# Expert tiles with two images' rows moved ahead in the last series, and their results turned beside the last tile

## The chip, the cores and the metric

The kernel runs on one core of a Trainium2 chip. The core has five engines that run side by side, each with its own queue of instructions: TensorE (PE, matmuls; PEld is its loading of weights), VectorE (DVE), ScalarE (ACT), GpSimd (POOL) and SyncE (SP). Transfers are issued from queues: SP's and ACT's go through the hardware queues, POOL's indirect ones through a software queue. The metric is the time of one execution on the device in microseconds, as a median over runs; less is better. The trace of one profiled execution shows where that time goes.

## What is computed

Four images of 256 channels and 32 x 32 positions pass through one layer: a mixer (selective scans, convolutions, attention) and then a mixture of experts over all 4096 positions (tokens). Only the second matters here:

```python
t = t + ffn(layernorm(t))              # t: 4096 rows of 256
# ffn, with 8 experts, two for each row:
gate_logits = xf @ Wg + bg
top_w, top_i = jax.lax.top_k(gate_logits, 2)
top_w = jax.nn.softmax(top_w, axis=-1)
for e in range(8):
    h = gelu(xf @ W1[e] + b1[e])       # 256 -> 1024
    out = out + w_dense[:, e:e+1] * (h @ W2[e] + b2[e])   # 1024 -> 256
```

All values are float32. The result goes back to the layout with the channels first.

## The kernel before

The images' mixers run one after the other. As each image is done, `dispatch` normalises its rows, picks the two experts of each and writes each row twice into a DRAM buffer XS, which has a region for every expert; a row of XS also carries its token's number and its weights. The rows before the experts are written to a second DRAM buffer, Y. XS grows by image, so the first rows of an expert's region are those of the earlier images.

The experts work by tiles of 256 rows of one expert. A plain tile loads its rows from XS and its expert's W1 and W2 (2 MB), turns the rows with four transposes on PE, and does 32 h matmuls (L2259) with a Gelu on ACT for each of eight blocks, then 32 y matmuls (L2272) in two row blocks of 128. DVE adds the bias (`ys`, L2286) and multiplies by the row's weight (L2291), and POOL adds each row block to its tokens' rows of Y with an indirect transfer that accumulates (L2299). The adds of a tile wait for those of the tile before it. A wide tile has 320 rows, in three blocks.

Tiles come in four series, `SERIES = (8, 8, 21, 8)`. Series 0 starts when two images' rows are counted, series 1 with three; both take whole tiles alone. Series 3 (`WIDE`) and series 2 (`rest`) come when all four images are counted: wide tiles take an expert's last rows, series 2 the plain tiles that are left. Which expert and which row each tile begins with is worked out on the chip by DVE in a table (`series` L2078, `wide_series` L2040, `table` L1991), and SP reads it into registers (`values_load`) ahead of each tile's loads. Of series 2 the last 9 tiles, of series 3 the last 4, are kept for rare splits of the rows: they stand in a conditional in `run` (L2141) and are skipped here. So 32 tiles run: 8, 8, and then a wide one followed by three plain ones, four times.

`tiles` (L1378) writes the order out by hand. The program is emitted step by step by generators (each `yield` lets the others emit), and each engine executes its instructions strictly in the order in which they were emitted. While tile n is emitted, `ahead(n + 1, at)` (L1438) is called at each of its steps: at step 0 it emits the table if it is wanted, the next tile's rows (L2160) and weights (L2194, L2196); from step 5 on, within the y matmuls, the next tile's transposes (`front`, L2218). Both tables of the last series are emitted in the first such call after image 3's places are known (L1440). Weights are held for two tiles.

After the last tile, `judge` (L1597) tests sums that the scans left, to decide on a second pass of the whole network (the conditional at L71, skipped here). Then `run` (L2113) opens a new pool, reads `any_late` into registers on all engines, skips the late tiles, and calls `bring_back` (L2310) for each of the four images: two loads of half an image from Y (L2315, 512 KB each), 16 transposes (L2324), eight copies out of PSUM shared by DVE (L2330) and ACT (L2328), and two stores to the output issued by ACT (L2331). Two `o` buffers are used in turn.

Of the kernel before, what the change touches and what calls it, by code (L numbers as in the profile page):

```python
# [14 lines left out]
P = 128  # L15
C = 256
# [32 lines left out]
LATE, LATE_WIDE = 9, 4  # L49

# [25 lines left out]
def network(  # L76
# [71 lines left out]
    with tc.tile_pool(name="w_conv", bufs=1) as wp, tc.tile_pool(  # L148
# [239 lines left out]
        def a8(name):  # L388
            return act8.tile([P, NC2, N], F32, tag="a8", name=name)
# [7 lines left out]
        def a4(name):  # L397
            return act4.tile([P, N], F32, tag="a4", name=name)
# [978 lines left out]

        def tiles():  # L1378
# [5 lines left out]
            between = (experts.SERIES[rest] - LATE) // some  # L1384
            for i in range(some):
                order.append((wide, i))
                order += [(rest, i * between + k) for k in range(between)]
# [50 lines left out]
            def ahead(n, at):  # L1438

                if experts.placed and wide not in tables:  # L1440
                    tables[wide] = experts.series(wide, temp)
                    tables[rest] = experts.series(rest, temp)
                if n == len(order):
                    return
                if n in got and len(got[n]) > 4:
                    return
                if n in xs and n in got and at >= 5:
                    front(n)
                    return

                if known(n) and n not in tables_of:
                    table(n)
                if n not in xs and sent(n):
                    rows(n)
                if n not in got and known(n):
                    load(n)

            for n in range(len(order)):
# [19 lines left out]
                for at, _ in enumerate(experts.tile(  # L1478
                    n, s, got[n], hs,
                    act4.tile([P, len(experts.blocks(s)), C], F32, tag="a4", name=f"ys_{n}"),  # L1480
                )):
                    if at < 4:
                        loaded[0] = None
                    ahead(n + 1, at)
                    yield T.get(("pace",), 1)
# [54 lines left out]
        with tc.manual_schedule(engines=ALL):  # L1540
# [53 lines left out]
            start(one_by_one(joined(B - 1), around(B - 1), sent_off(B - 1)))  # L1594
            drain()

    if not shifted:  # L1597
        with tc.tile_pool(name="judge", bufs=1) as jp:
            most = jp.tile([P, 1], F32, name="most")
            for i, span in enumerate((SPAN, INVERSE)):  # L1600
                nc.vector.tensor_scalar(sums[:, i, :], sums[:, i, :], span, None, ALU.is_lt)
            nc.vector.tensor_reduce(most, sums.rearrange("p a b -> p (a b)"), AX.X, ALU.min)

            nc.vector.tensor_scalar(most, most, 1.0, None, ALU.is_lt)
            any_ = ps_tile("any")
            nc.tensor.matmul(any_[0:1, 0:1], ones_mean[:, 0:1], most, start=True, stop=True)
            nc.vector.tensor_scalar(bad, any_[0:1, 0:1], 0.0, None, ALU.is_gt)

    experts.run(experts.tables)
# [11 lines left out]
class Experts:  # L1621
# [19 lines left out]
    def __init__(self, ctx, tc, psum, B, b1, ident, eps5, ones_mean, Wg, bg, W1, W2, b2, out):  # L1641
# [74 lines left out]
        self.read = []  # L1716
        self.apart = m0.tile([P, 1], F32, name="apart")
# [249 lines left out]
    def count_up(self, s, temp):  # L1967

        nc, K, n = self.nc, self.NTOK // self.T, self.SERIES[s]
        steps = temp(f"steps_{s}", [P, NE, K])  # L1970
        base = {self.WIDE: 0, self.WIDE - 1: REST}.get(s, self.T - 1)
        nc.gpsimd.iota(
            steps, [[0, NE], [self.T, K]], base=base,
            channel_multiplier=0, allow_small_or_imprecise_dtypes=True,
        )
        which = temp(f"which_{s}", [P, n, NE])
        nc.gpsimd.iota(
            which, [[1, n], [0, NE]], base=0, channel_multiplier=0,
            allow_small_or_imprecise_dtypes=True,
        )  # L1980
        self.numbers[s] = steps, which

# [8 lines left out]
    def table(self, temp, keep, name, n, ntile, which, done=None):  # L1991
# [3 lines left out]
        ends = keep(f"ends_{name}", [P, 1, NE])  # L1995
        nc.vector.tensor_tensor_scan(
            ends[:, 0, :], self.every[:, 0:NE], ntile[:, 0, :], 0.0, ALU.mult, ALU.add
        )
        starts = temp(f"starts_{name}", [P, 1, NE])
        nc.vector.tensor_tensor(starts, ends, ntile, ALU.subtract)  # L2000
        S = [P, n, NE]
# [7 lines left out]
        nc.vector.tensor_scalar(expert, expert, float(NE - 1), None, ALU.min)  # L2009
# [7 lines left out]
        nc.vector.tensor_tensor(which, which, self.region[:, 0:1, :].to_broadcast(S), ALU.add)  # L2017
# [13 lines left out]
    def use(self, s, ends):  # L2031

        late = LATE_WIDE if s == self.WIDE else LATE
        over = self.used[s] = self.m0.tile([P, 1], mybir.dt.int32, name=f"over_{s}")
        self.nc.vector.tensor_scalar(
            over, ends[:, :, NE - 1 : NE].rearrange("p a e -> p (a e)"),
            float(late - self.SERIES[s]), 0.0, ALU.add, ALU.max,
        )

    def wide_series(self, temp):  # L2040
# [34 lines left out]
        self.use(s, ends)  # L2075
        return table

    def series(self, s, temp):  # L2078
# [7 lines left out]
        if s == self.WIDE - 1:  # L2086
            assert before + n == self.NTILE
            table, _, ends = self.table(temp, self.kept, s, n, self.left, which, self.done)
            self.use(s, ends)
            self.any_late = self.m0.tile([P, 1], mybir.dt.int32, name="any_late")  # L2090
            nc.vector.tensor_tensor(
                self.any_late, self.used[s], self.used[self.WIDE], ALU.add
            )
            return table
# [18 lines left out]
    def run(self, tables):  # L2113

        tc, nc = self.tc, self.nc
        with tc.tile_pool(name="moe2", bufs=2) as m2:
            def load(v):
                return nc.values_load(
                    v[0:1, 0:1], min_val=0, max_val=sum(self.SERIES),
                    skip_runtime_bounds_check_because="made from counts of at most NTOK rows",  # L2120
                )

            def late_tile(s, i):
                j, W = f"{s}_{i}", self.width(s)
                w1 = m2.tile([P, NC2, DFF], F32, tag="w1", name=f"w1_{j}")
                w2 = m2.tile([P, NHC, C], F32, tag="w2", name=f"w2_{j}")
                got = self.load(
                    s, i, tables[s], [w1], [w2], m2.tile([P, C], F32, tag="b2", name=f"b2_{j}")
                )
                xs = m2.tile([P, len(self.blocks(s)), self.ROW], F32, tag="xs", name=f"xs_{j}")  # L2130
                self.rows(s, i, tables[s], xs)
                got += self.front(
                    j, s, i, tables[s], xs, m2.tile([P, NC2, W], F32, tag="xT", name=f"xT_{j}")
                )
                for _ in self.tile(
                    j, s, got, [m2.tile([P, NHC, W], F32, tag="hs", name=f"hs_{j}")],
                    m2.tile([P, len(self.blocks(s)), C], F32, tag="ys", name=f"ys_{j}"),
                ):
                    pass

            with tc.If(load(self.any_late) > 0):  # L2141
                for s, late in ((self.WIDE - 1, LATE), (self.WIDE, LATE_WIDE)):
                    n = self.SERIES[s]
                    with tc.If(load(self.used[s]) > 0):
                        for i in range(n - late, n):
                            late_tile(s, i)
            for b in range(self.B):
                self.bring_back(b, m2)
# [96 lines left out]
    def tile(self, j, s, got, hs, ys):  # L2245
# [9 lines left out]
        for k0 in range(0, NHC, each):  # L2255
# [9 lines left out]
            if k0 % 2 == 0:  # L2265
                yield
        for t, n in blocks:
            if t % 2 == 0:
# [9 lines left out]
            if parts > 1:  # L2278
# [3 lines left out]
                nc.vector.tensor_tensor(ys[0:n, t], yp[0:n, 0:C], other, ALU.add)  # L2282
            elif t % 2 or t == len(blocks) - 1:
# [6 lines left out]
        for t, n in blocks:  # L2290
            nc.vector.tensor_scalar(  # L2291
                ys[0:n, t, :], ys[0:n, t, :], wgt[0:n, t, :], None, ALU.mult
            )

        added = []
        for t, n in blocks:
            if t:
                nc.gpsimd.memset(self.apart, 0.0)
            ins = nc.gpsimd.indirect_dma_start(  # L2299
                out=self.Y[:, :],  # L2300
                out_offset=bass.IndirectOffsetOnAxis(ap=dest[0:n, t, :], axis=0),
                in_=ys[0:n, t, :], in_offset=None, compute_op=ALU.add,
            )
            for other in added:
                self.tc.declare_no_dep(ins.ins, other.ins, reason="no two share a row")
            self.follow(ins, self.added, "a row may be added to by both")
            added.append(ins)
        self.added = added

    def bring_back(self, b, m2):  # L2310

        nc, NT = self.nc, self.NT
        y = m2.tile([P, NT, C], F32, tag="yy", name=f"yy_{b}", bufs=self.B)
        for h in range(2):
            nc.sync.dma_start(  # L2315
# [3 lines left out]
        o = m2.tile([P, NC2, N], F32, tag="o", name=f"o_{b}")  # L2319
# [112 lines left out]
```

## Time and profile before

| what | us |
|---|---|
| median of three runs | 2202.95 |
| lowest, highest | 2195.85, 2204.05 |
| the profiled execution | 2182.24 |
| its span, first to last instruction | 2180.3 |
| PE busy | 1937.3 (89%) |
| DVE busy | 1533.4 (70%) |
| ACT busy | 1212.4 (56%) |
| POOL busy | 1048.1 (48%) |

The span is what the trace covers; the execution is 1.9 us longer. PE's busy time contains pipelined matmuls. A time such as 2151.22 is counted from the span's start. In a timeline a line has the start, the length, the engine, the line of the code, the operation and its tiles, how many in a row, and in brackets how long the engine had been idle and what released it. "SPq" and the like are the instructions of an engine's queue (issues of transfers, semaphores, branches), which are not counted as busy.

### The profile page before, as it was taken

How to read it: one execution, taken by the hardware profiler on the slowest of the kernel's cores; microseconds unless marked ns; L12 is line 12 of the kernel's file. 1: busy time of each engine (PE TensorE's matmuls, PEld its weight loads, DVE VectorE, ACT ScalarE, POOL GpSimd, SP SyncE). 2: the span in 40 equal slices, each digit the busy share in tenths (PEclk: the TensorE clock that was granted, in tenths of full speed). 3: DMA queues.
4: the chain of work that ended last, by engine and by line, in shares of the span. 5: the costliest groups of instructions: out<-in, count | busy, mean ns of one | idle time of the engine just before them, and what ended most of it. 6: DMA issues, size and time to landing. Idle time of an engine off the chain costs nothing. (4 is left out here: it accounts for less than half of the span.)

```text
span 2180.3 us, 28168 instructions
## 1 busy us (share of the span) xinstructions
PE 1937.3 (89%) x8690; PEld 874.4 (40%) x8690; DVE 1533.4 (70%) x2231; ACT 1212.4 (56%) x2272; POOL 1048.1 (48%) x930
## 2 busy tenths in 40 slices
PE   6778778999978999987789999768999999999995
PEld 2113112322212332222123223225642668888884
DVE  4989998857999988799898888985365356121211
ACT  4665657668668577776566776625168423222221
POOL 0887887712888740476977025752040013422221
PEclk8988999999999999998999999889999999999997
DMA  3565553401444421153634024454230166967665
GB/s 107 146 162 123 127 125 91 106 22 59 116 115 107 111 60 39 34 132 100 177 79 113 1 78 101 104 177 123 78 115 1 46 196 198 261 186 191 175 162 167
DMA packets 157087, 251.40 MB, mean 115 GB/s; under 512 B 34740, under 2 KB 101332, under 8 KB 156664
## 3 DMA queue, kind: packets, MB, share of 16 engines
q1 hardware_dynamic: 136560, 223.47, 37.8%
q0 software_dynamic: 12720, 17.32, 4.0%
q10 hardware_dynamic: 7640, 8.65, 1.2%
q8 instruction: 72, 1.18, 0.2%
q14 instruction: 95, 0.78, 0.1%
HBM read 137.22 MB, written 36.62 MB: 80 GB/s over the span
## 5 line engine op out<-in xcount | busy, mean ns | idle before, releaser
L744 POOL TENSOR_TENSOR dA<-hs,cs 128x512 f32<-128x512 f32 x512 | 683.2, 1342 | 374.8 <-DVE hs L736 315.8
L715 ACT ACTIVATE dA<-dts,A 128x512 f32<-128x512 f32 x512 | 358.7, 718 | 159.2 <-DMA dts<-dt 71.8
L754 PE MATMUL yp<-dA,quads 128*32 128x512 f32 x1024 | 290.0, 640 | 85.3 <-POOL dA L744 74.0
L2299 POOL DMA_INDIRECT Y<-ys,dest x68 | 108.8, 1601 | 507.6 <-DVE ys L2291 500.2
L1133 ACT ACTIVATE e<-st 128x512 f32<-128x512 f32 x512 | 263.8, 605 | 93.2 <-PE st L1123 85.8
L2264 ACT ACTIVATE hs<-h,b 128x256 f32<-128x256 f32 (+1 forms) x256 | 110.5, 478 | 334.7 <-PE h L2259 231.7
L725 DVE TENSOR_TENSOR dBu<-dts,bs 128x512 f32<-128x512 f32 x384 | 260.0, 678 | 49.8 <-PE bs L707 14.8
L736 DVE TENSOR_TENSOR_SCAN hs<-dA,last,dBu 128x512 f32<-128x512 f32 x192 | 243.7, 1269 | 3.3 <-PE yp L754 1.1
L2272 PE MATMUL y<-w,hs 128*128 128x256 f32 (+1 forms) x1088 | 244.6, 384 | 0.0
L2259 PE MATMUL h<-xT,w 128*128 128x256 f32 (+1 forms) x1024 | 237.4, 388 | 0.1
L736 DVE TENSOR_TENSOR_SCAN hs<-dA,dBu 128x512 f32<-128x512 f32 x192 | 232.0, 1208 | 3.7 <-PE av L1143 2.7
L1179 DVE TENSOR_TENSOR e<-e,e 128x512 f32<-128x512 f32 x256 | 170.0, 726 | 76.0 <-ACT e L1133 40.2
L2272 PEld LDWEIGHTS y<-w,hs 128*128 128x128 f32 (+1 forms) x1088 | 199.1, 190 | 36.3 <-issue 8.7
L2259 PEld LDWEIGHTS h<-xT,w 128*128 128x128 f32 x1024 | 194.5, 191 | 43.6 <-issue 11.0
L2222 DVE COPY xT<-xp 128x512 f32<-128x512 f32 (+1 forms) x36 | 23.3, 646 | 245.5 <-PE xp L2218 245.2
L707 PE MATMUL bs<-u,xpwT_s 128*32 128x512 f32 x1024 | 162.8, 652 | 34.9 <-DVE hs L736 15.1
L1123 PE MATMUL st<-qk 32*128 32x512 f32 x1024 | 174.8, 638 | 1.9 <-DVE hs L736 1.9
L754 PEld LDWEIGHTS yp<-dA,quads 128*32 128x32 f32 x1024 | 51.1, 114 | 298.1 <-POOL dA L744 194.1
L1169 PE MATMUL av<-e,v 128*32 128x512 f32 x1024 | 138.6, 604 | 0.0
L1123 PEld LDWEIGHTS st<-qk 32*128 32x128 f32 x1024 | 59.9, 183 | 116.7 <-issue 86.2
L1143 PE MATMUL av<-e,every 128*32 128x512 f32 x512 | 86.8, 594 | 4.1 <-DVE e L1179 4.1
L725 DVE TENSOR_TENSOR bs<-dts,bs 128x512 f32<-128x512 f32 x128 | 86.2, 674 | 0.7 <-DMA dts<-dt 0.7
(335 smaller groups left out, 2625.0 us busy)
## 6 DMA issues: line engine op xcount, KB each, us to landing
dts<-dt SPq DMA_DIRECT2D x512, 128.0 KB, 2.4
w<-in_W_dram SPq DMA_DIRECT2D x124, 512.0 KB, 3.9
cs<-cd SPq DMA_DIRECT2D x512, 64.0 KB, 2.1
xs<-XS SPq DMA_DIRECT2D x32, 260.0 KB, 4.2
xd<-xn SPq DMA_DIRECT2D x64, 128.0 KB, 3.0
xn<-in_x_dram SPq DMA_DIRECT2D x8, 512.0 KB
XL<-xl SPq DMA_DIRECT2D x8, 512.0 KB
xl<-XL SPq DMA_DIRECT2D x4, 1024.0 KB
```

Source lines behind the costliest of these rows:

```text
L707: nc.tensor.matmul(bs[r], xpwT_s[:, n, s : s + 1].to_broadcast([P, 32]), T[b, n, "u"][:, half(h)], start=True, stop=True,)
L715: nc.scalar.activation(dA, T[b, n, h, "dts", g][:, 0, :], AF.Exp, scale=A[:, g, n, q : q + 1])
L725: nc.vector.tensor_tensor(dBu, T[b, n, h, "dts", g][:, 1, :], T[b, n, h, "bs", q], ALU.mult)
L736: nc.vector.tensor_tensor_scan(hs, T[b, n, h, "dA", i], dBu, 0.0 if h == 0 else last, ALU.mult, ALU.add)
L744: nc.gpsimd.tensor_tensor(dA, hs, T[b, n, h, "cs", q], ALU.mult)
L754: nc.tensor.matmul(T[b, n, h, "yp"][ts(g, 32)], quads, T[b, n, h, "dA", q * GD + g], start=False, stop=(q == GS - 1),)
L1123: nc.tensor.matmul(sts[i], k[r, ts(kt, P)], q[r, half(h)], start=True, stop=not shifted)
L1133: nc.scalar.activation(es[i], sts[i], AF.Exp, scale=1.0 / HD**0.5)
L1169: nc.tensor.matmul(accs[0][ts(i, HD)], v8[:, kt, ts(4 * g + i, HD)], es[i], start=(kt == 0), stop=(kt == NK - 1),)
L1179: nc.vector.tensor_tensor(first[i], first[i], es[i], ALU.add)
L2259: nc.tensor.matmul(hp[:, i, :], w1(c, k0 + i), xT[:, c, :], start=(c == 0), stop=(c == NC2 - 1))
L2272: nc.tensor.matmul(yp[ts(k % parts, n), ts(t % 2, C)], hidden(k)[:, ds(t * P, n)], w2(k), start=(k < parts), stop=(k >= NHC - parts),)
```

## The change

The order of the last series is another: the first wide tile, then eight plain ones in a row (`EARLY = 8`), then four times a plain one after which, but for the last, a wide one comes. The eight are meant to hold all rows of images 0 and 1 (`SOON = 2`) that are left by then, so series 2 now ranks its tiles by two kinds for each expert: those with rows of the first two images, then the others. The table works with 16 kinds in place of 8. It is emitted in the call that follows the first wide tile's rows, and no longer beside the wide table. At the fifth step of the second tile after the eight (tile 26 of 0 to 31), images 0 and 1 are loaded from Y. They are turned and stored after the last tile and ahead of the conditional. If more than eight tiles turn out to hold such rows, a count `redo` makes the conditional load and turn the two again. The last tile weighs and adds each of its row blocks as soon as its own y matmuls are done (`apart`). The judging is emitted among the tiles. The new pool is gone; its tiles come from the pools in use, which have eight buffers of an image's size.

```diff
+EARLY, SOON = 8, 2
...
+            order += [(wide, 0)] + [(rest, i) for i in range(EARLY)]
+            final = len(order)
+            between = (experts.SERIES[rest] - LATE - EARLY) // some
             for i in range(some):
-                order.append((wide, i))
-                order += [(rest, i * between + k) for k in range(between)]
+                order += [(wide, i)] * (i > 0)
+                order += [(rest, EARLY + i * between + k) for k in range(between)]
...
                 if experts.placed and wide not in tables:
                     tables[wide] = experts.series(wide, temp)
+                if wide in tables and rest not in tables and order[n - 1] == (wide, 0):
                     tables[rest] = experts.series(rest, temp)
...
                     ahead(n + 1, at)
+                    if n == final + 1 and at == 4:
+                        for b in range(SOON):
+                            experts.fetch(b, a8(f"yy_{b}"))
...
+            if not shifted:
+                start(judged())
             drain()
+            for b in range(SOON):
+                experts.turn(b, a8(f"o_{b}"))
+
+        experts.run(experts.tables, a8, a4, a2)
```

In the table, ranks over 7 stand for the second kind of an expert:

```diff
+        if kinds > NE:
+            second = temp(f"second_{name}", [P, n, 1])
+            nc.vector.tensor_scalar(
+                second, expert, float(NE), float(-NE), ALU.is_ge, ALU.mult
+            )
+            nc.vector.tensor_tensor(expert, expert, second, ALU.add)
...
+            nc.vector.tensor_tensor(first, self.soon, self.done, ALU.subtract)
+            nc.vector.tensor_scalar(first, first, 0.0, None, ALU.max)
+            nc.vector.tensor_tensor(first, first, self.left, ALU.min)
+            nc.vector.tensor_tensor(second, self.left, first, ALU.subtract)
...
+            nc.vector.tensor_scalar(
+                over, ends[:, 0, NE - 1 : NE], float(-EARLY), 0.0, ALU.add, ALU.max
+            )
+            self.redo = self.m0.tile([P, 1], mybir.dt.int32, name="redo")
+            nc.vector.tensor_tensor(self.redo, over, self.missed, ALU.add)
```

The wide table also counts, for each expert, how many tiles the first two images' rows reach into (`soon`), and how many of them a wide tile would hold (`missed`). In the last tile:

```diff
+            elif apart:
+                nc.vector.tensor_tensor(ys[:, t], yp[:, ts(t % 2, C)], b2_s, ALU.add)
+                weigh(t, n)
+                add(t, n)
```

And the end, where `fetch` has the two loads and `turn` the transposes, copies and stores of what was `bring_back`:

```diff
+        with tc.If(load(self.any_late) > 0):
...
+            with tc.If(load(self.redo) > 0):
+                for b in range(SOON):
+                    self.fetch(b, a8(f"yy_{b}_again"))
+                    self.turn(b, a8(f"o_{b}_again"))
+        for b in range(SOON, self.B):
+            self.fetch(b, a8(f"yy_{b}"))
+        for b in range(SOON, self.B):
+            self.turn(b, a8(f"o_{b}"))
```

## The prediction

> **What bounds the kernel now.** I read three views, in this order: the busy time by stretch of the span, the timeline of the end, and the semaphore instructions that stand at a skipped branch. The stretches come first. Columns: length, then busy us and count for PE, PEld, DVE, ACT and POOL, the granted clock, the DMA share, GB/s.
>
> ```profile
> 1897.00:2142.70 245.70, 245.70 (x1159) 205.76 (x1158) 45.90 (x151) 58.57 (x132) 58.53 (x56) 1.00 0.62 167
> 2142.70:2180.30 37.60, 11.61 (x66) 10.52 (x64) 6.63 (x12) 4.69 (x8) 3.23 (x3) 0.62 0.71 234
> ```
>
> From the first wide tile to the last expert tile PE never rests, at full clock: nothing put there can shorten that stretch, only lengthen it. The last 37.6 us hold 11.6 us of PE. They are the only stretch the change can shorten. The timeline of the end says what they consist of:
>
> ```profile
> 2135.54 7.07 PE L2272 MATMUL y<-w,hs 128*128 128x256 f32 x32
> ...
> 2144.00 1.56 POOL L2299 DMA_INDIRECT Y<-ys,dest  x1 [10.38 <-DVE ys L2291]
> 2144.98 0.69 POOL L2298 MEMSET apart<- 128x1 f32 x1
> 2145.86 1.56 POOL L2299 DMA_INDIRECT Y<-ys,dest  x1 [0.19 <-POOLq L2141]
> 2151.22 7.77 SPq L2315 DMA_DIRECT2D yy<-Y  x8
> 2155.74 7.30 PEld L2324 LDWEIGHTS op<-ident,yy 128*128 128x128 f32 x40 [13.12 <-POOLq L71]
> ...
> 2162.40 0.59 ACT L2328 COPY o<-op 128x512 f32<-128x512 f32 x1 [0.66 <-PE op L2324]
> ...
> 2170.70 1.94 PE L2324 MATMUL op<-ident,yy 128*128 128x128 f32 x8 [2.42 <-SPq L71]
> ...
> 2173.70 0.50 ACTq L2331 DMA_DIRECT2D out_dram<-o  x1
> ```
>
> Call E the end of the last y matmul, about 2142.65. The second add starts at E+3.2, the loads of Y at 2151.22 = E+8.6, the first transposes 4.5 us later; the eighth half image arrives at 2170.70 (19.5 us after the first issue), the last store is issued at 2173.70 (3.0 later) and the span ends 6.6 us after that. E to the end is 37.65 us. The third view is the two conditionals, L2141 (late tiles) and L71 (the whole network again), both skipped:
>
> ```profile
> L71 SPq EVENT_SEMAPHORE  x9: 17/17/17, 2165.5 to 2178.5; - x9
> ```
>
> ```profile
> L2141 SPq EVENT_SEMAPHORE  x9: 17/17/17, 2120.5 to 2121.1; - x9
> L2141 POOLq EVENT_SEMAPHORE  x6: 17/30/43, 2145.7 to 2149.8; - x6
> ...
> L2141 PEldq COMPARE_BRANCH  x1: 3351/3351/3351, 2139.6 to 2139.6; - x1
> ...
> L2141 POOLq INC_SWDGE_SEM  x1: 986/986/986, 2149.9 to 2149.9; - x1
> ```
>
> At a skipped branch SP goes through nine semaphores. At L2141 this took 0.6 us, since only weights had been in flight. At L71 it took 13 us, until 2178.5: by 2170.7 all loads of Y had arrived, so what was left to wait for were the stores that ACT had issued. SP passes a skipped branch only when all earlier transfers of both hardware queues have landed. POOL's pair ends at 2150.9, 0.3 us before SP's loads.
>
> [...] the trace has 0.22 us at 64 and 0.33 at 168 elements[...]. [...] after an idle 4.20 us, sixteen y matmuls took 5.84 us and not 3.62. [...]
>
> **The change part by part.**
>
> *Order.* 32 tiles before and after, the same kinds, a plain one last. PE's matmuls are the same: 0.
>
> *Fetch of images 0 and 1 beside tile 26.* SP waits for tile 25's adds; at the end of before that wait was 8.6 us after the y matmuls. Then four of the eight loads, half of 7.77 us: SP is free 12.5 us after tile 25. Queued behind are the rows and weights of tile 28, wanted after a wide tile (17.9 us, 1897.47 to 1915.40) and a plain one (14.25, 2114.38 to 2128.63), so 19.7 us later. 2 MB at the 350 GB/s of the end's loads take 6 us, inside that. Tile 26's adds wait for these loads (landed about 19 us after tile 25; the adds are due at 17.9+1.4). Cost 0; without the cover some 3 us. Bounds 0 and 3.
>
> *Wide table.* The first burst of DVE (1842.5 to 1853.2) loses the ordered table (4.2 us, 1849.02 to 1853.2) and gains about ten short operations, two over 128 elements (0.29 each), 2.3 us together. PE waited 0.14 us there. Gain 0.1, taken as 0.
>
> *Ordered table behind the first wide tile's rows.* Its DVE operations now stand after tile 15's ys and weighting, which ended at 1899.0, and tile 17's rows and weights in SP's queue stand behind the table. Before, those rows were issued at 1885.21. The table is 16 kinds wide, so 336 elements: 0.51 us an operation, an estimate [...]. Six short ones (1.2), scan and starts (0.35), three at 0.51, a sum and three short ones (1.05), two at 0.51, a scaling (0.36), two halves of the region at 0.39, one at 0.51, a sum and two casts (0.83): 7.6 us, ready at 1906.7. The same step is in the trace for the series before: table ready 1749.57, rows issued 1750.69, transposes 1753.58, so 1.1 + 2.9. Here: 1910.7. PE wants the rows at 1909.6 (after sixteen y matmuls, 1906.08+3.62). Stall 1.1 us. Bounds: 0, if the table takes 6.5; 2.6, if the rows take the 4.4 of the DMA view. First weights follow the rows by 0.95 and are wanted 5.7 us after them; at the earlier place 8.5 us were enough and no wait showed. I take 1.1.
>
> *Judging moved.* Four DVE operations and two one-column matmuls (0.19 us) leave E and enter a time when DVE is half idle: 0.
>
> *Last tile block by block.* The first block's add is issued while the second's y matmuls run. After E: one sum and one weighting (0.35 each), one add. It starts at E+0.8, not E+3.2; with 3.85 us to land (2145.86 to POOL's 2149.7) and POOL's 1.2, Y is ready at E+5.9, not E+8.3. That only counts if nothing else holds SP.
>
> *Turns of images 0 and 1 at E.* 32 warm transposes beside the last add, 1.06 us for eight. ACT paces them: copy 0.59 and a store's issue 0.4 to 0.5, so 1.1 us a half. First store at E+1.85, fourth at E+5.15. The conditional L2141 now comes after them, with these four stores in flight. The last store of before was issued at 2173.70 and SP's last wait ended at 2178.5: 4.8 us. So SP passes its nine at E+9.95 and issues the loads at F = E+10.3, not E+6.2. PE (3.35 us at the branch), DVE (2.9) and ACT (up to 3.8 at L71) pass theirs by E+9, E+9 and E+10.4: near F, but none waited for alone. The 2.4 us won by the last tile's blocks lie under this wait.
>
> *Two images at the end.* The first four halves of before are the pattern: loads at 2151.22, the fourth ACT copy at 2162.40, ended 2162.99. So the last store is issued at F+11.85. (Before, it had to wait: only two o buffers. Now there are eight.) With 6.6 us after it: E+10.3+11.85+6.6 = E+28.75. Against 37.65: 8.9 us won. Bounds: F between E+9 and E+11.
>
> *Sum.* 8.9 − 1.1 = 7.8 us. The profiled execution has 2180.3 us of span and 2182.24 in all, so 2174.4. The median of the runs shown, 2202.95, is 20.7 us above that execution; I carry the difference over: 2195.1.
>
> **The rivals.** *SP isn't held* (the waits at the skipped branch are over sooner, or the landing takes 2 us): F = E+6.2 and 13.0 − 1.1 = 11.9 us won, 2191.0. For it: at L2141 nothing waited before. Against it: L71. *The late table costs as much as the one at 1749*: 4.2 us idle and 2.2 + 0.5 lost to the half clock, 6.9 in all; 8.9 − 6.9 = 2.0 won, 2201.0. Against it: DVE has nothing else to do at 1899. *The late table costs more than the end brings* (the other side): operations twice as dear (15.3 us) and rows at 4.4 give 1919.9, a stall of 10.3, with 2.7 for the clock 13: 4.1 lost, 2207. It decides once tile 17's rows arrive over 9 us late, after 1918.6. *The early results aren't used*: if more than eight ordered tiles hold rows of images 0 and 1, both are loaded and turned again. Counted from the reference's own routing, six tiles do and none is missed. It would cost the whole tail of before and some 8 us: 2212.
>
> **How the numbers follow.** Forecast 0.46, SP not held 0.32, a table like at 1749 0.11, the slower one 0.07, no use 0.04. A measurement of this kernel can tell about 0.5% (11 us) from no change; the three runs lie within 8.2 us. With 6 us of spread about a third of the forecast's chance and 0.6 of the second case pass 11 us: 0.16 + 0.19 + 0.01 = 0.36. Slower by 11 us takes a part of the last two and what I haven't seen: 0.07. Same: 0.57. The range goes from the second case less 6 us to just short of the slower one: 2185 to 2206.
>
> **What would show it.** Right: PE without a gap from 1897 on, but for about 1 us ahead of tile 17's transposes; transposes within 0.5 us of the last y matmul; loads of Y some 10 us after it, behind SP's nine semaphores, and not 6; E to the end 28 to 29 us. Wrong: loads at E+6 (then 2191); a gap over 3 us at tile 17, with slow matmuls after it; gaps around tiles 26 to 28; transposes of images 0 and 1 twice.

## The result and the profile after

| | before | after |
|---|---|---|
| median us (22 runs each) | 2202.49 | 2195.09 |
| lowest, highest | 2195.85, 2208.0 | 2188.61, 2201.88 |
| the profiled execution | 2182.24 | 2195.89 |
| its span | 2180.3 | 2194.1 |
| E, the end of the last y matmul | 2142.61 | 2164.31 |
| E to the end | 37.66 | 29.77 |

The ratio is 0.997, interval [0.9961, 0.9979]: 7.4 us are won, the forecast was 7.8. The change is real but under the 0.5% that the prediction called distinguishable in one measurement.

The two profiled executions can't be subtracted from each other. The one of before was quicker than every timed run of before, and was so ahead of the last series: from the first h matmul of all to E it took 689.1 us, the one of after 707.7. Run e3 below, which keeps the order and the end of before but for the last tile, took 707.7 as well. So these 18.6 us belong to that execution, and only stretches that begin at a matmul close by are compared here. The first view of after is the busy time by stretch, with the columns of the prediction; the stretches are from the first wide tile to E, and from E to the end.

```profile
1918.98:2164.31 245.33, 245.33 (x1157) 205.19 (x1156) 53.62 (x181) 58.56 (x132) 60.29 (x58) 1.00 0.66 181
2164.31:2194.10 29.79, 9.19 (x65) 8.24 (x62) 6.12 (x10) 4.69 (x8) 1.57 (x1) 0.75 0.67 225
```

The stretch of the experts is as long as before (245.70 there) and as full: the new order, the fetch beside tile 26, the late table and the moved judging cost it nothing. All that is won stands in the second line. Its timeline:

```profile
2157.24 7.07 PE L2361 MATMUL y<-w,hs 128*128 128x256 f32 x32
...
2164.15 3.66 PE L2408 MATMUL op<-ident,yy 128*128 128x128 f32 x32
...
2165.44 1.57 POOL L2346 DMA_INDIRECT Y<-ys,dest  x1 [1.77 <-DVE ys L2339]
2165.89 0.39 ACTq L2415 DMA_DIRECT2D out_dram<-o  x1
...
2169.02 0.58 ACTq L2415 DMA_DIRECT2D out_dram<-o  x1
2175.17 2.08 SPq L2395 DMA_DIRECT2D yy<-Y  x4
...
2179.15 3.50 PE L2408 MATMUL op<-ident,yy 128*128 128x128 f32 x16 [11.35 <-DMA yy<-Y]
...
2186.81 0.38 ACTq L2415 DMA_DIRECT2D out_dram<-o  x1
```

The 32 transposes of images 0 and 1 follow the last y matmul with no gap. The last add starts at E+1.1, where it was E+3.2; the four stores are issued from E+1.6 to E+4.7. Then SP issues nothing until E+10.86. What it waits for shows at the skipped conditional, L2204 here:

```profile
L2204 SPq EVENT_SEMAPHORE  x9: 17/17/17, 2138.5 to 2174.8; - x9
...
L2204 PEldq COMPARE_BRANCH  x1: 4794/4794/4794, 2166.3 to 2166.3; - x1
...
L2204 POOLq INC_SWDGE_SEM  x1: 986/986/986, 2171.7 to 2171.7; - x1
```

The last of the nine is passed at 2174.8, the moment at which the fourth store has landed (2174.83, E+10.5). At the same place in before this line ended at 2121.1, 21 us ahead of E.

### The profile page after: what moved, and what is told of

Its sections match the earlier page's. It is cut to its first block, busy times and chain, and to the rows that moved or that the text cites. A ratio compares the mean times of both kernels' runs of the same rounds, so it can differ in the third digit from the quotient of the medians.

```text
span 2194.1 us, 28173 instructions
## 1 busy us (share of the span) xinstructions
PE 1943.7 (89%) x8690; PEld 872.0 (40%) x8690; DVE 1538.8 (70%) x2252; ACT 1211.9 (55%) x2272; POOL 1047.5 (48%) x931
## 3 DMA queue, kind: packets, MB, share of 16 engines
q1 hardware_dynamic: 136560, 223.47, 36.5%
## 5 line engine op out<-in xcount | busy, mean ns | idle before, releaser
L2291 DVE COPY xT<-xp 128x512 f32<-128x512 f32 (+1 forms) x36 | 23.2, 646 | 236.3 <-PE xp L2287 236.0
L1126 PE MATMUL st<-qk 32*128 32x512 f32 x1024 | 180.6, 644 | 8.5 <-issue 6.6
```

The source lines that it names most:

```text
L1126: nc.tensor.matmul(sts[i], k[r, ts(kt, P)], q[r, half(h)], start=True, stop=not shifted)
```

## Experiments

Ten runs were made, in three groups, each beside its own runs of before, so ratios are compared rather than times. Eight are of other kernels; e10 and e12 are the changed kernel again. The table collects them. E is the end of the last y matmul of each profile; the next columns count from it. "Transfers" is the number of 512 KB transfers, loads of Y and stores, still to be made from the first one that SP issues behind the last add.

| run | median us | ratio to before | loads | last store issued | end | transfers | first of them to the end |
|---|---|---|---|---|---|---|---|
| before | 2202.49 | | 8.6 | 31.1 | 37.7 | 16 | 29.0 |
| after | 2195.09 | 0.997 [0.9961, 0.9979] | 10.9 | 22.5 | 29.8 | 8 | 18.9 |
| e1_stores_behind | 2195.11 | 0.9959 [0.9945, 0.9972] | 6.6 | 23.2 | 30.4 | 12 | 23.9 |
| e2_table_early | 2199.94 | 0.9989 [0.9976, 1.0003] | 10.8 | 21.0 | 28.2 | 8 | 17.4 |
| e3_before_apart | 2200.36 | 0.9991 [0.9982, 1.0] | 6.5 | 30.2 | 36.5 | 16 | 30.0 |
| e4_after_whole | 2195.95 | 0.9975 [0.9962, 0.9988] | 12.9 | 23.8 | 31.3 | 8 | 18.4 |
| e8_one_early | 2197.56 | 0.9963 [0.9948, 0.9978] | 8.3 | 20.4 | 28.5 | 11 | 21.6 |
| e9_behind_loads | 2197.83 | 0.9975 [0.9962, 0.9989] | 7.4 | 21.8 | 29.3 | 12 | 22.5 |
| e6_not_stored | 2190.48 | 0.9946 [0.9928, 0.9963] | 7.0 | 17.9 | 25.7 | 8 | 18.7 |
| e10_after_again | 2196.30 | 0.9964 [0.995, 0.9979] | 11.0 | 21.5 | 28.8 | 8 | 17.8 |
| e11_loads_ahead | 2198.76 | 0.9985 [0.9973, 0.9997] | 7.1 | 25.5 | 31.9 | | |
| e12_after_third | 2196.44 | 0.9965 [0.995, 0.9979] | 10.8 | 21.7 | 28.7 | 8 | 17.9 |

Before ran at 2202.51 beside e1 to e4, at 2203.92 beside e6 to e10, at 2202.53 beside the last two. The three profiles of after end at E+29.8, 28.8 and 28.7, so a single tail says nothing on differences under about 1 us.

### e1: the stores behind the conditional

`turn(..., False)` transposes and copies without storing; `turned` are tiles that live across the branch. The four stores are cut by channels here, and in e8 and e9, where after cuts them by positions; the bytes are the same.

```diff
-                experts.turn(b, a8(f"o_{b}"))
+                experts.turn(b, turned[b], False)
...
         for b in range(SOON, self.B):
             self.fetch(b, a8(f"yy_{b}"))
+        for b in range(SOON):
+            for c in range(NC2):
+                nc.scalar.dma_start(self.out[b, ts(c, P), :], turned[b][c])
```

> The changed kernel, but images 0 and 1 are only turned ahead of the conditional, into buffers of the weights' pool; their four stores are issued behind it. Counted from E, the end of the last y matmul. Theory (SP is held at the skipped conditional by the four stores): its semaphores no longer stop, the loads of images 2 and 3 go out at about E+7 and not E+11.0, held by the last add and by PE's branch; the end comes at E+26 to E+28 against E+29.9, the loads now sharing the transfers with the stores, so 2 to 4 us faster than the changed kernel, 0.995 to 0.996 of before. Rival (the last add, slowed by traffic, holds the loads in any case): loads at E+10 or later and the end within 1 us of E+29.9.

SP is no longer held; its line at the skipped conditional (L2208 in this kernel) ends well ahead of E = 2165.43:

```profile
L2208 SPq EVENT_SEMAPHORE  x9: 17/17/17, 2139.2 to 2139.8; - x9
...
L2208 POOLq INC_SWDGE_SEM  x1: 986/986/986, 2170.9 to 2170.9; - x1
```

The timeline of the same kernel's end has both queues after the branch:

```profile
2165.26 3.66 PE L2415 MATMUL op<-ident,yy 128*128 128x128 f32 x32
...
2171.98 4.13 SPq L2402 DMA_DIRECT2D yy<-Y  x4
2172.20 3.64 ACTq L2222 DMA_DIRECT2D out_dram<-o  x4
2177.73 1.94 PE L2415 MATMUL op<-ident,yy 128*128 128x128 f32 x8 [8.81 <-DMA yy<-Y]
...
2183.35 4.58 PE L2415 MATMUL op<-ident,yy 128*128 128x128 f32 x24 [3.68 <-DMA yy<-Y]
```

The loads start at E+6.6 instead of E+10.9, and the end does not come sooner: 30.4. The stores now go out at the same moment as the loads; PE has the first half at E+12.3 and then waits for the second until E+17.9. That SP's hold at the branch comes from the stores is shown. That it costs what it lasts, 4.3 us, is not. The theory had the loads right, at about E+7, and the end wrong, at E+26 to E+28; the rival had the loads at E+10 or later. The question of the later runs is what takes the hold's place.

The stores delay the loads in two ways. In e1 the loads follow POOL's last step at the branch, which ends at E+6.5, once the last add has landed. In after this step ends only at E+8.4, as the add lands later among the stores; from there to E+10.9 SP's semaphores alone hold the loads.

### e2: the ordered table beside the wide one

```diff
-                if wide in tables and rest not in tables and order[n - 1] == (wide, 0):
+                if wide in tables and rest not in tables:
```

> The changed kernel with the ordered table emitted beside the wide table, as before the change. Theory (the table is only free where DVE has nothing behind it): DVE's burst after the places are known gets 7.5 us longer than in the changed kernel, the next tile's xT copy waits for it, and PE stands still for 5 to 7.5 us in front of that tile's h matmuls, with slow matmuls after it: about 5 to 9 us slower than the changed kernel, level with before. The 0.14 us in front of tile 17's transposes go. Rival (the place of the table is without effect, as the prediction took the first burst for nothing): within 1 us of the changed kernel.

TensorE in the tile where both tables are made, and the tile after it for comparison:

```profile
1872.36 3.62 PE L2361 MATMUL y<-w,hs 128*128 128x256 f32 x16
1882.19 9.54 PE L2328 MATMUL h<-xT,w 128*128 128x256 f32 x32 [6.21 <-DVE xT L2291]
...
1898.91 7.07 PE L2328 MATMUL h<-xT,w 128*128 128x256 f32 x32
```

The next tile's `xT` copy stands behind the table in DVE's queue, PE is idle for 6.21 us, and the 32 matmuls after that take 9.54 us, not 7.07: 8.7 us lost. In after, the same table stands here:

```profile
1927.59 3.62 PE L2361 MATMUL y<-w,hs 128*128 128x256 f32 x16
1931.18 0.66 PE L2287 MATMUL xp<-ident,xs 128*128 128x128 f32 x4
1931.68 5.50 PE L2361 MATMUL y<-w,hs 128*128 128x256 f32 x32
```

The transposes of tile 17 follow the first sixteen y matmuls; they start 3.59 us after these, where before has 3.45, so 0.14 us late. So the place of the table is worth most of what the change brings: with it at the early place the ratio is 0.9989, with an interval that contains 1, against 0.9959 and 0.9975 of e1 and e4, which ran beside it with the table late. (Their medians differ from it by 4 to 5 us rather than by 8.7; the intervals are 5 to 6 us wide.)

### e3 and e4: the last tile block by block, added alone and taken away

e3 is before with `tile` as in the change, and the argument `apart` true for the last tile:

```diff
+                    n == len(order) - 1,
```

e4 is after with that argument false:

```diff
-                    n == len(order) - 1,
+                    False,
```

> The kernel before with one part of the change alone: the last tile weighs and adds block by block. Theory: there nothing but the last add holds the loads of Y, so they go out at about E+6.2 and not E+8.6, and the end comes 2.4 us sooner (37.65 to about 35.3 us after E), 0.999 of before. Rival (the branches of the conditional hold the loads): loads stay at E+8 or later, no gain.

> The changed kernel with the last tile weighed and added as a whole, as before. Theory (the block by block adds lie under SP's wait for the stores): the last add starts 2.4 us later, the loads of images 2 and 3 still go out at E+11 to E+12, and the end is within 1 us of E+29.9. Rival (the add holds the loads): they go out 2.4 us later, at E+13.4, and so does the end.

In before, the blocks alone bring the loads from E+8.6 to E+6.5 and the end from E+37.7 to E+36.5, half of the 2.4 us that were expected; the time, 0.9991, can't be told from 1. In after, taking them away delays the loads as well, from E+10.9 to E+12.9, and the end to E+31.3, which is nearer to the rival than to the theory. The timeline of e4 shows why they do not vanish behind the stores:

```profile
2169.58 1.57 POOL L2346 DMA_INDIRECT Y<-ys,dest  x1 [8.15 <-DVE ys L2339]
2170.25 0.39 ACTq L2415 DMA_DIRECT2D out_dram<-o  x1
...
2171.45 1.57 POOL L2346 DMA_INDIRECT Y<-ys,dest  x1 [0.19 <-POOLq L2204]
...
2173.37 0.55 ACTq L2415 DMA_DIRECT2D out_dram<-o  x1
2181.03 2.08 SPq L2395 DMA_DIRECT2D yy<-Y  x4
```

Both adds now lie among the stores, the stores start 0.5 us later because DVE's sums come first, and the fourth store lands at E+12.5 instead of E+10.5. In time the difference of e4 to after is not resolved (0.9975 against 0.997).

### e8, e9 and e6: the stores behind the loads, or not at all

In e9 the four stores of e1 go to SP's queue, behind the loads. In e8 the first of them is issued when image 0 has been turned, ahead of the conditional, and three stand behind the loads. In e6 the four are left out, and with them two images of the output.

e9 against e1:

```diff
-                nc.scalar.dma_start(self.out[b, ts(c, P), :], turned[b][c])
+                nc.sync.dma_start(self.out[b, ts(c, P), :], turned[b][c])
```

e6 against after:

```diff
+            if b >= SOON:
                 nc.scalar.dma_start(
```

> The changed kernel with images 0 and 1 turned where they are, but only the first of their four 512 KB stores issued there; the other three go to the same queue as the loads of images 2 and 3, behind these. E is the end of the last y matmul; in the changed kernel the loads start at E+11.0 and the end is at E+29.8. Theory one (SyncE held at the conditional sets the end): loads at E+7, and the rest follows as in the changed kernel, 18.9 us from the loads to the end: E+25.9, total near 2191. Theory two (the half-megabyte transfers set it, some 1.4 us each when the DMA engines are full): from the loads on 11 transfers instead of 8, so 7 + 3 to the first landing + 11 x 1.4 + 2.1 = E+27.5, total near 2193.

> As the run with one store early, but all four stores of images 0 and 1 stand behind the loads of images 2 and 3 on the loads' queue. Theory one: loads at E+6.6, end at E+25.5, total near 2191. Theory two: 12 transfers from the loads on, 6.6 + 3 + 12 x 1.4 + 2.1 = E+28.5, total near 2194. The kernel with these stores on ScalarE's queue beside the loads had its loads at E+6.6 and its end at E+30.4.

> The changed kernel without the four stores of images 0 and 1 (these results are left out of the output). Nothing holds SyncE but the last add: both theories want the loads at E+6.5 and, with 8 transfers behind them as in the changed kernel, the end at E+25.4, total near 2191. If the loads start later than E+8, it is not the stores that hold SyncE. If the end is later than E+27, something else than loads and stores sets it.

> The changed kernel once more, beside these three: 2195, ratio 0.997 to before, the end at E+30 with the loads at E+11. If the tail of another execution differs by over 1.5 us from 29.8, single tails can't be told apart by less than that.

In both e8 and e9 the order that came out has one of SP's stores ahead of the loads, not all behind; the transfers are as many as planned. In e9, with loads at E+7.4, the end is at E+29.3, where the hold alone would have given 25.5 and the count of transfers 28.5. e8 comes to 28.5, against 25.9 and 27.5. Only leaving the stores out gives the 25.7 that a start of the loads at E+7 promised. So it is not SP that is short of time. The DMA view shows it: each digit is the busy share of the 16 engines, in tenths, in one of 40 slices of the stretch from E to the end. Before, in slices of 0.94 us:

```profile
DMA  0004757000289999999999999999998189997000
```

After, in slices of 0.75 us:

```profile
DMA  9206999999993100599999998960299999120000
```

e9, in slices of 0.73 us:

```profile
DMA  8200691000598999998899999999999999721000
```

e6, in slices of 0.64 us:

```profile
DMA  9300197100005499998899897449999981200000
```

In before only the two adds use them until the loads come, some 10 us after E. In after the engines are full with the four stores while SP is held (slices 5 to 12), have one pause of some 3 us (slices 13 to 16: SP's release and the loads' way), and are full again but for a dip ahead of the last stores. In e9 the pause has moved ahead of the transfers (slices 7 to 10), and these then run without one for 24 slices of 0.73 us: 17.6 us for 12 transfers. In e6 there is simply less. The last two columns of the table give the price. With 8 transfers to go, the end comes 17.4 to 18.9 us after the first (mean of six 18.2); with 11 after 21.6; with 12 after 22.5 and 23.9; with 16 after 29.0 and 30.0. Between 8 and 16 that is (29.5 − 18.2)/8 = 1.41 us for each half megabyte, or 372 GB/s, an estimate from these tails; in before the engines moved 363 GB/s from 2154.00 to 2170.70, a stretch in which they were full. Between 8 and 12 alone it is (23.2 − 18.2)/4 = 1.25 us. Single tails scatter by more than a microsecond, so 1.2 to 1.4 us is what these runs support.

This also says where the 7.9 us between the two tails come from. From E on, before has 16 of these transfers to make and after 12, since four loads went beside tile 26: an estimate of 5 to 5.6 us from the price above. The rest is that four stores use a time in which the DMA engines of before have only the two adds. No run takes the two apart.

### e11: the loads ahead of the conditional

`last` holds buffers of the weights' pool for images 2 and 3, which no later tile uses.

```diff
+        any_late = load(self.any_late)
+        for b in last:
+            self.fetch(b, last[b])
-        with tc.If(load(self.any_late) > 0):
+        with tc.If(any_late > 0):
...
+            for b in last:
+                self.fetch(b, last[b])
```

> The changed kernel with the loads of images 2 and 3 issued ahead of the conditional, into buffers of their own, so that SyncE no longer has to pass its nine semaphores first; the late tiles, if there are any, load them again. Nothing is left out. The four stores of images 0 and 1 stay where they are, so the DMA engines should work without the gap of some 3 us that stands at E+11 to E+14 in the changed kernel. If the transfers set the end: loads issued at E+7, when the last add has landed; the eight transfers land by E+16, some 1.3 us apart; the last store is issued near E+17.5 and the end is at E+24, total near 2190. If the hold is only moved, because the other engines cannot use the loads until SyncE has passed the branch with all of them landed: transposes start at E+16, the end is at E+28, total near 2194.

> The changed kernel beside the run with the loads ahead: 2195 to 2196, ratio 0.997, the loads at E+11 and the end at E+29 to E+30.

This was to close the pause. SP at the skipped conditional, L2211 here:

```profile
L2211 SPq EVENT_SEMAPHORE  x9: 17/17/17, 2179.2 to 2180.5; - x9
...
L2211 SPq COMPARE_BRANCH  x1: 50/50/50, 2173.7 to 2173.7; - x1
```

And the loads and PE's transposes of images 2 and 3 in the timeline:

```profile
2169.53 3.74 SPq L2403 DMA_DIRECT2D yy<-Y  x4
2180.53 5.58 PE L2416 MATMUL op<-ident,yy 128*128 128x128 f32 x32 [14.62 <-SPq L2211]
```

The second theory written down for this run holds, though its transposes at E+16 and its end at E+28 came 2 and 4 us later. The loads are issued at E+7.1, and the DMA engines carry the eight transfers without a pause until about E+17.5, slice 22 of 40 slices of 0.80 us from E on:

```profile
DMA  8108999999997889999731000008919899950000
```

But PE, which stands behind the branch, does not start until SP has gone through its nine semaphores, at E+18.1, within 0.1 us of it. SP itself reached the branch at 2173.7 and had its first semaphore 5.5 us later. The end comes at E+31.9, 2 to 3 us later than in the three profiles of after, and the ratio is 0.9985 against 0.9965. Of the arrangements that ran with all work in place, none beats the changed kernel by more than the measurements can tell.

## Why the prediction was right, step by step

*The stretch of the experts.* Cost 0 was taken for the order, the fetch beside tile 26 and the judging; 245.33 us against 245.70, and PE dense throughout. Right.

*The ordered table.* Predicted 7.6 us of DVE and a stall of 1.1, bounds 0 to 2.6; measured 7.05 us and 0.14. The length of one operation at 336 elements, an estimate of 0.51 that continues the 0.22 at 64 and the 0.33 at 168 elements of before, was 0.50 to 0.51; the sum of the short ones was too high by half a microsecond, and the transposes came 2.7 us behind the rows, not 2.9. (The sum 1906.08 + 3.62 for the moment at which PE wants the rows is 1909.7, not 1909.6; the transposes of before began at 1909.53.) The rivals that made this table dear are refuted for this place, the early results were used (the two images are turned once), and e2 shows that they would have been right at the other: idle 6.2 us, and 2.5 lost in slower matmuls, where the 1749 rival had 4.2 and 2.7. At the rival's place in before, behind the idle 4.20 us, the granted clock was 0.50 over the four transposes (1753.58 to 1754.48) and 0.60 over the sixteen y matmuls of 5.84 us; how long an idle it takes is not shown.

*SP is held at the branch.* The mechanism was read from the old L71 and it is what happened, down to the kind and number of the instructions: SP passed when the last store had landed, at 2178.5 in before (landed 2178.49) and at 2174.8 in after (2174.83). The fourth store was issued at E+4.7 rather than E+5.15 and took 5.8 us to land rather than 4.8, so F is E+10.86 and not E+10.3. The bounds E+9 to E+11 held it.

*The two images at the end.* From F the last store was to be issued 11.85 us later (11.77 by the two lines it names); it was 11.63. The 6.6 us behind it were 7.3. E+28.75 was forecast, and three profiles show 29.8, 28.8 and 28.7.

*The sum.* 8.9 − 1.1 = 7.8 was forecast. The mean tail of the three profiles is 29.1, so 8.6 us are won there, 0.14 lost at tile 17: 8.4 by the profiles, 6.1 to 7.6 by the differences of medians of the three sets of runs of after. The size of the end was met, the stall was overestimated, and the two errors are smaller than the scatter of a median. The tail of before is that of one profile. That 2195.1 was forecast and 2195.09 measured is luck: the interval of the ratio leaves 4.6 to 8.6 us.

*Two things the prediction had wrong.* "The 2.4 us won by the last tile's blocks lie under this wait": e4, one profile, shows 2.0 of them at the loads and 1.5 to 2.6 at the end. The likely reason is that the adds share the DMA engines with the stores that SP waits for; it is not tested alone. The last add took 6.1 us to land among the stores, not 3.85; without them (e6) it took 4.3. And the rival *SP isn't held*, 0.32 and 2191.0, stood on a step that e1, e8 and e9 refute: that the end follows the start of the loads at a fixed distance. With loads at E+6.6 to E+8.3 the end stays at E+28.5 to 30.4. The forecast's own sum took the same step; it held there because the four stores had landed, at E+10.5, before the loads went out, so that eight transfers alone were left. The hold is where four transfers are made; whoever removes the hold and keeps the transfers pays for them among or behind the loads. The forecast was right about the hold and silent on why it costs so little.

What stays open: whether the pause of 3 us in after can be closed by a store order that e8 and e9 didn't reach, and the 0.8 to 2.3 us by which the differences of medians lie below the 8.4 of the profiles.

## What to carry to other kernels

Before shortening a wait at the end of a kernel, count the bytes that have yet to move and divide by the rate of a full stretch: if the DMA engines are full during the wait, as here, removing it only moves the transfers (e1 and e9 removed it, and their ends, E+30.4 and E+29.3, are within 0.6 us of the E+29.8 of after). Transfers that can be made while computation lasts, here the loads of two images, are worth what they take out of the tail, by these runs some 1.2 to 1.4 us for each half megabyte. And work on a control path (a table) that is too dear in one place may cost nothing one tile later, where its engine idles (8.7 us in e2, 0.14 in after); look for the slack of the engine that it queues on, not for the earliest moment at which its inputs exist.

## What the runs showed of the hardware

- At a skipped branch of these programs SP passed only when the transfers issued before it had landed. In before (L71) it passed at 2178.5, when the last store had landed (2178.49); in after at 2174.8, when the fourth store had (2174.83); in e1, with no store ahead of the branch, at 2139.8, long before E. PE, behind the branch, waited for SP's pass where it needed loads issued ahead of it (e11: the first load was issued at 2169.53, SP passed at 2180.5, E+18.1, and the transposes began at 2180.53, 11.0 us behind that load; in after they began 4.0 us behind the first load).
- Passing a skipped branch took microseconds. From SP's comparison to its first semaphore it was 3.6 to 4.1 us at this conditional in nine profiles (before, after, e1 to e4, e6, e8, e9), well ahead of E, and 5.5 in e11, with loads in flight. At the next one it was 6.1 us in before (L71) and 5.5 in after (L74), with transfers in flight. PE is less clear: 4.8 us in three profiles with the four stores in flight (after, e2, e11) and 3.35 to 3.75 in five without stores (before, e1, e3, e6, e9), with 3.99 for one store (e8), but also 3.35 in e4, with stores just begun, and 3.59 at L71 of before, amid loads and stores. What lengthens it is not shown.
- Indirect adds landed later among ordinary stores: 6.1 us after issue in after, and 6.0 in e11 and, with one store, in e8, against 3.8 to 4.3 without (before, e1, e3, e6, e9).
- How long SP takes to issue varies: four loads took it 2.08 us in after and 4.13 in e1, where ACT issued four stores at the same moment. That is not all of it: it was 2.77 us in e6, where ACT issued none beside them, and 3.74 in e11, behind the stores.
